# Two macaron layers on one core: softmax division moved ahead of the transposes in the second attention, and the last mixture-of-experts stage reordered

## The chip, the cores and the metric

The kernel runs on one core of a Trainium2 chip. Its engines are TensorE (PE, matrix products and transposes into PSUM), VectorE (DVE), ScalarE (ACT), GpSimd (POOL, which here also issues the indirect DMAs) and SyncE (SP, which issues plain DMAs). Each engine works through its own instruction queue in order; semaphores hold an instruction until what it reads is there. The metric is the device time of one execution in microseconds (us), lower is better.

## The reference, cut to what matters

Input x is 8 x 512 tokens of 256 float32 values. Six residual steps follow each other, each on the layer norm of x; the change lies in the last two.

```python
x = x + 0.5 * _L0_ffn_ref(_layernorm(x), ...)
x = x + _L0_attn_ref(_layernorm(x), ...)
x = x + 0.5 * _L0_ffn_ref(_layernorm(x), ...)
x = x + 0.5 * _L1_ffn_ref(_layernorm(x), ...)
x = x + _L1_attn_ref(_layernorm(x), ...)
x = x + 0.5 * _L1_ffn_ref(_layernorm(x), ...)

def _L1_attn_ref(x, w_q, w_k, w_v, w_o):        # 16 heads of 64
    q, k, v = (einsum('bsd,hdk->bhsk', x, w) for w in (w_q, w_k, w_v))
    weights = softmax(einsum('bhqk,bhmk->bhqm', q, k) / 8, axis=-1)
    z = einsum('bhqm,bhmk->bhqk', weights, v)
    return x + concat_heads(z) @ w_o

def _L1_ffn_ref(x, gate_w, w1, w2, w3, ws1, ws2, ws3):
    scores = softmax(x @ gate_w.T)              # 16 experts in 4 groups
    # the two best groups by their best score, then the four best experts in them
    y = sum over the 4 experts e of scores[e] * (silu(x @ w1[e]) * (x @ w3[e])) @ w2[e]
    return y + (silu(x @ ws1) * (x @ ws3)) @ ws2
```

## The kernel before, in words

x stays in SBUF as 32 tiles of 128 tokens (`TT` = 32); four tiles (`QT`) are one sequence of 512 tokens. `D` = 256, `CH` = 512. Both stages below are scheduled by hand: the order in which the Python emits instructions is the order in each engine's queue.

**Second attention (`_attn1`, 2174 to 3409 us).** 64 chunks `n`, each two heads of one sequence (`b, c = divmod(n, 8)`). The loop runs over half chunks `g`; each emits, in this order: the scaling of the chunk before (`scale`), the transposes of two exponential tiles of the half before (`turn`, L1130, four transposes each into a PSUM bank of tag "m", evicted to `eT` by ScalarE for the first head and VectorE for the second), some pieces of side work from the list `todo` (layer norms, gathers and additions of the FFN before, routing of the FFN after), one of the q or k projections of the next chunk (`side`, L1088), two more `turn`s, then `scores`, and then a filler (`fill`): `products` of the chunk before (L1157) in the first half, and in the second half value projections (`value`, L1077), output projections (`project`, L1172), the transposed input of the next sequence (`columns`) or gate logits of the next FFN. `scores` makes two PSUM tiles of 128 x 1024 (L1110), negates the row maximum on VectorE (L1116), and lets ScalarE write the exponentials `ex` and their row sums (L1119). The division comes last: `reciprocals` takes 1/sum, ScalarE spreads it over 64 columns for each head (`wide`, L1138), `spread` transposes that with four TensorE transposes (L1144) and copies it to `rs` (L1148), and `scale` multiplies the product `zp` by `rs` (L1164). Tag "m" has three banks, used in turn by tp, pq, pv, yp, rp and the gate's tiles.

**Last FFN (`ffn1_after`, class `Joint`, from the attention's end).** `LAST` = 20, 12: the routing of the first 20 token tiles (part 0) is done inside the attention, as pieces; their rows are sent by GpSimd (`send`, L1857, four indirect DMAs a tile) into slots ordered by expert. The other 12 tiles (part 1) are routed at the start of this stage: tiles 20 to 27 have their logits from the attention, tiles 28 to 31 (group g = 7) get norm, transposes (`columns`) and `logits` first. `routing` is a generator; `advance(steps, n)` emits up to n of its pieces, and a piece that yields "turn" ends the call. After it, 48 sends for part 1.

The expert work is a pipeline of 72 entries of two slot tiles (`tile_steps`): at step i it emits `hide(i-2)` (L2073), `back(i-3)` (L2087), `turn(i)` (L2058) and `give(i-4)` (L2095), with evictions alternating between VectorE and ScalarE, a load of `xs` from the slots (L2040) and a store of `ys` (L2103). The first 32 entries hold rows of part 0 alone, the others wait for all sends. Expert weights are picked by a register, so a `hide` waits for all of w13. From step `begin` on, `fetched` emits the combination: GpSimd gathers four rows a token (`gather`, L2010, four a tile, buffers for four tiles in all, then a memset of `pause`), and VectorE adds them to x with the coefficients (`add`, L1614), three tiles behind the gather. After the steps a `Pump` runs the shared expert in 32 units (two hidden and two output units for each group of four tiles) and spreads the remaining half tiles of `fetched` over them. A tile of x goes out once both parts are added.

`expert_weights` loads w1, w3 and w2 by groups of four experts through SP; w1 and w3 land interleaved in `w13`, in pieces of 128 values (512 bytes). `ln_root` takes the norm's square root on ScalarE, `ln_guess` by arithmetic on VectorE.

Of the kernel before, what the change touches and what calls it, by code (L numbers as in the profile page):

```python
# [19 lines left out]
P = 128  # L20
# [49 lines left out]
class Kernel:  # L70
# [124 lines left out]
    def ln_guess(self, pool, stats, t0, n):  # L195

# [11 lines left out]
        for i in range(3):  # L208
            u = small("u")
            nc.vector.tensor_tensor(u, y, y, ALU.mult)  # L210
            nc.vector.scalar_tensor_tensor(u, u, -0.5, v, ALU.mult, ALU.mult)
            new = stats[1][:, t0 : t0 + n] if i == 2 else small("y", bufs=2)
            nc.vector.scalar_tensor_tensor(new, u, 1.5, y, ALU.add, ALU.mult)
            y = new

# [820 lines left out]
    def _attn1(self, ctx, weights, one, after):  # L1036
# [61 lines left out]
        def scores(n, half):  # L1098
# [4 lines left out]
            sps = []  # L1103
# [9 lines left out]
            for i, sp in enumerate(sps):  # L1113
# [3 lines left out]
                ex = ch["ex", qt] = work.tile([P, 2, CH], F32, name="ex", bufs=4)  # L1117
                for j in range(2):
# [3 lines left out]
                    )  # L1122

# [9 lines left out]
        def reciprocals(n):  # L1133
            ch = chunk[n]
            rec = work.tile([P, QT, 2], F32, name="rec", bufs=2)
            nc.vector.reciprocal(rec, ch["sums"])
            ch["wide"] = work.tile([P, QT, 2, DK1], F32, name="wide", bufs=1)
            nc.scalar.copy(ch["wide"], bc(rec, 3, DK1))  # L1138

        def spread(n):  # L1140
            ch = chunk[n]
            rp = bank("rp")
            for qt in range(QT):
                nc.tensor.transpose(  # L1144
                    rp[:, qt * P : qt * P + P], ch["wide"][:, qt].rearrange("p h d -> p (h d)"), self.ident
                )
            ch["rs"] = work.tile([P, CH], F32, name="rs", bufs=1)
            nc.scalar.copy(ch["rs"], rp)  # L1148
# [13 lines left out]
        def scale(n):  # L1162
            zn = work.tile([P, CH], F32, name="zn", bufs=11)
            nc.vector.tensor_tensor(zn, chunk[n]["zp"], chunk[n]["rs"], ALU.mult)  # L1164
# [29 lines left out]
        def roots(ranges):  # L1194
            ys = []

            def first():
                for stats, t0, n in ranges:
                    ys.append(self.ln_root(pool, stats, t0, n))

            def second():
                for (stats, t0, n), y in zip(ranges, ys):
                    self.ln_rest(pool, stats, t0, n, y)
            return [first, second]
# [75 lines left out]
        side(0, 1)  # L1280
        for g in range(2 * N + 1):
# [3 lines left out]
            if half == 0 and n < N:  # L1285
                todo += listed(n)
            if half == 1 and n > 0:
                scale(n - 1)
            if g > 0:
                turn(m, 2 * mh, 0)  # L1290
                turn(m, 2 * mh, 1)
            if half == 0 and n > 0:
                reciprocals(n - 1)
            pieces(1)
            if n + 1 < N:
                side(n + 1, half)
# [3 lines left out]
            if half == 0 and n > 0:  # L1300
                spread(n - 1)
            if n < N:
                scores(n, half)
# [8 lines left out]
                for piece in fill(n, half):  # L1312
                    piece()
            else:
                products(n - 1)
        scale(N - 1)
# [4 lines left out]
        for i in range(QT):  # L1321
            project(B - 1, i)
            self.ln_mean(self.late, after.stats, (B - 1) * QT + i)

# [137 lines left out]
class Grouped:  # L1462
# [194 lines left out]
    def expert_weights(self, groups=range(4)):  # L1657
        nc, w = self.k.nc, self.k.w
        for g in groups:
            es = slice(g * 4, g * 4 + 4)  # L1660
            nc.sync.dma_start(
                out=self.w13[:, es, :, 0:INTER], in_=w["w1"][es].rearrange("e (c p) i -> p e c i", p=P)
            )
            nc.sync.dma_start(
                out=self.w13[:, es, :, INTER:], in_=w["w3"][es].rearrange("e (c p) i -> p e c i", p=P)
            )
            nc.sync.dma_start(out=self.w2[:, es], in_=w["w2"][es].rearrange("e p d -> p e d"))
# [160 lines left out]
class Joint(Grouped):  # L1828
# [23 lines left out]
    def send(self, h, t, row):  # L1852
# [3 lines left out]
        for r in range(TOPK):  # L1856
# [6 lines left out]
            before = self.sent[-2:-1]  # L1863
# [6 lines left out]
            self.of_part[h].append(inst)  # L1870

    def routing(self, h, lg, pool, row_psum):
# [3 lines left out]
        HT = self.parts[h]  # L1876
        GS = E1 // N_GROUPS

        score = pool.tile([P, HT, E1], F32, name="score")
# [21 lines left out]
        hots = pool.tile([P, TOPK, HT, E1], F32, name="hots")  # L1901
        yield from k.topk(pool, masked, E1, TOPK, hots)

        chosen = pool.tile([P, E1, HT], F32, name="chosen")
# [9 lines left out]
        carry = pool.tile([P, E1, HT], F32, name="masked")  # L1914
# [5 lines left out]
        inc = pool.tile([P, E1, HT], F32, name=f"left{E1}")  # L1920
# [103 lines left out]
    def tile_steps(self):  # L2024
# [25 lines left out]
        def turn(j):  # L2050
# [9 lines left out]
            k.evict(st[j]["xT"][:, :n], tp[:, :n], j)  # L2060
# [22 lines left out]
        def back(j):  # L2083
# [5 lines left out]
            k.evict(st[j]["aT"][:, :n], tp[:, :n, :P], j)  # L2089

        def give(j):
# [9 lines left out]
            k.evict(ys[:, :n], yp[:, :n], j + 1)  # L2101
# [12 lines left out]
        return load, step, len(where) + 4, known  # L2114

# [181 lines left out]
def ffn1_after(k, f, out):  # L2297
# [4 lines left out]
    with ExitStack() as ctx, k.tc.manual_schedule(engines={E.PE, E.DVE, E.Activation, E.Pool, E.SP}):  # L2302
        f.enter(ctx)
        a = f.parts[0]
        load, step, total, known = f.tile_steps()
        f.expert_weights(range(1))
        for j in range(4):
            load(j)
        f.expert_weights(range(1, 4))
        f.shared_weights()  # L2310
        g = TT // QT - 1
        for i in range(3):
            step(i)
        k.ln_guess(f.route, f.stats, g * QT, QT)
        f.normal(g)
        f.columns(g)
# [3 lines left out]
        steps = f.routing(1, f.lg1, f.route, f.row_psum)  # L2320
# [20 lines left out]
        begin, at, ends = known + 3, 0, 2 * (len(order) + 3)  # L2341
        rest = list(range(g)[::-1])
        for i in range(total):
            if i >= 3:
                step(i)
            if not sending:
                sending = not advance(steps, 4)
                if i < 2:
# [140 lines left out]
```

## Time and profile before

| what | us |
|---|---|
| runs: median of 3 (lowest, highest) | 3820.96 (3817.65, 3825.62) |
| profiled execution | 3822.71 |
| its span | 3821.0 |
| TensorE, VectorE, ScalarE, GpSimd busy | 3583.2, 1860.9, 1451.8, 1244.2 |
| second attention | 2174 to 3409 |
| last FFN, expert steps | 3409 to 3705 |
| last FFN, shared expert and rest of the gathers | 3705 to 3821 |

How to read it: the span is the profiled execution without what lies around it (1.7 us). A busy time is the union of an engine's instructions; matrix products are pipelined, so the time that one takes from the queue is read from start to start. In a windows view each line gives a stretch, its length, each engine's busy time with the number of instructions, the TensorE clock that was granted (1.00 is full), the DMA engines' share and GB/s. In a timeline a line gives start, length, engine, source line, operation, tiles, and in brackets the idle time before it with what ended it.

### The profile page before, as it was taken

What the parts mean: (1) busy time and instruction counts of PE and PEld (TensorE: products, weight loads), DVE (VectorE), ACT (ScalarE), POOL (GpSimd) and SP (SyncE); (2) the same over time, 40 slices, a digit from 0 to 9 for tenths busy, and PEclk for the clock granted to TensorE, in tenths of its full rate; (3) what the DMA queues carried; (4) which work ended last, traced back from release to release, by engine and by line L of the source; (5) the groups of instructions that cost most, each with busy time, mean ns of one, the idle gap of its engine ahead of it and who ended that gap; (6) DMA issues with size and microseconds to landing.
All of it is one profiled execution on the core that took longest, in us unless ns stands there. A gap on an engine that the chain in (4) does not pass through costs nothing.

```text
span 3821.0 us, 51805 instructions
## 1 busy us (share of the span) xinstructions
PE 3583.2 (94%) x18293; PEld 2235.2 (58%) x18293; DVE 1860.9 (49%) x4500; ACT 1451.8 (38%) x2922; POOL 1244.2 (33%) x1142
## 2 busy tenths in 40 slices
PE   4999999999996899998989999999999999988988
PEld 1566664555553566666678745555555555557865
DVE  6212205665655312116535566666556567546355
ACT  3222223444444222221123355555555555532321
POOL 2333235343331333333763312220000002714177
PEclk7999999999998899998999999999999999999989
DMA  5355442000113233324467401000000000135564
GB/s 194 97 139 146 109 103 85 23 18 23 29 34 96 49 69 78 71 41 134 135 219 236 135 18 31 28 26 1 1 1 1 1 1 23 72 113 185 163 182 130
DMA packets 258173, 309.32 MB, mean 81 GB/s; under 512 B 34048, under 2 KB 227968, under 8 KB 257664
## 3 DMA queue, kind: packets, MB, share of 16 engines
q1 hardware_dynamic: 182144, 177.78, 14.8%
q0 software_dynamic: 49152, 101.24, 10.7%
q10 hardware_dynamic: 26624, 27.00, 2.1%
q8 instruction: 151, 2.47, 0.3%
q14 instruction: 102, 0.84, 0.1%
HBM read 159.51 MB, written 138.02 MB: 78 GB/s over the span
## 4 chain that ended last, share of the span: by engine, by line
PE 37%; issue 8%; POOL 6%; DMA 2%; DVE 1%; ACT 0%; POOLq 0%; DVEq 0%; SPq 0%; ACTq 0%
PE sp L1110 6%; PE tp L1130 6%; PE pq L1088 6%; PE zp L1157 6%; PE pv L1077 3%; PE yp L1172 3%; POOL slots_d L1493 3%; PE hs L1786 2%; POOL yg L2010 2%; PE hs L2073 1%; PE yps L1808 1%; POOL slots_d L1857 1%; PE rp L1144 1%; DMA yg<-ys_d,slot 1%; PE yps L2095 1%
## 5 line engine op out<-in xcount | busy, mean ns | idle before, releaser
L521 PE MATMUL hp<-exT,w 128*128 128x512 f32 x1024 | 453.4, 597 | 0.7 <-DVE exT L509 0.7
L552 PE MATMUL op<-w,hid 128*128 128x256 f32 x2048 | 451.9, 379 | 0.0
L1119 ACT ACTIVATE ex<-sp,nmax 128x512 f32<-128x512 f32 x512 | 345.1, 686 | 238.8 <-DVE nmax L1116 238.7
L552 PEld LDWEIGHTS op<-w,hid 128*128 128x128 f32 x2048 | 386.8, 190 | 64.1 <-issue 14.4
L557 DVE TENSOR_TENSOR ob<-op,b 128x256 f32<-128x256 f32 x128 | 54.4, 425 | 642.8 <-PE op L552 555.3
L1116 DVE TENSOR_REDUCE nmax<-sp 128x2 f32<-128x1024 f32 x256 | 301.6, 1220 | 81.4 <-PE sp L1110 81.4
L531 POOL DMA_INDIRECT acc_d<-ob,idx x128 | 201.7, 1576 | 419.3 <-ACT ob L558 353.2
L812 DVE CUSTOM_DVE_ANT_0 junk<-sp,mask 128x128 bf16<-128x128 f32 (+3 forms) x512 | 251.2, 491 | 166.4 <-PE sp L803 142.3
L521 PEld LDWEIGHTS hp<-exT,w 128*128 128x128 f32 x1024 | 192.8, 191 | 221.5 <-issue 216.7
L1130 PEld LDWEIGHTS tp<-ident,ex 128*128 128x128 f32 x2048 | 233.8, 141 | 144.7 <-issue 84.7
L525 ACT ACTIVATE hid<-hp,b 128x512 f32<-128x512 f32 x256 | 175.9, 687 | 317.0 <-PE hp L521 317.0
L1130 PE MATMUL tp<-ident,ex 128*128 128x128 f32 x2048 | 272.9, 275 | 6.6 <-ACT ex L1119 4.1
L1110 PE MATMUL sp<-qk,qk 64*128 64x512 f32 x1024 | 254.4, 615 | 0.0
L1601 POOL DMA_INDIRECT yg<-ys_d,slot x128 | 129.6, 1013 | 359.2 <-DVE x L1614 267.0
L1088 PE MATMUL pq<-xnT,wide 128*128 128x512 f32 x512 | 244.1, 600 | 1.2 <-ACT xnT L250 0.8
L252 DVE COPY eT<-tp 128x512 f32<-128x512 f32 x256 | 177.1, 692 | 138.7 <-PE tp L1130 138.5
L1157 PE MATMUL zp<-eT,v 128*64 128x512 f32 x1024 | 234.0, 598 | 0.0
L250 ACT COPY eT<-tp 128x512 f32<-128x512 f32 x256 | 149.8, 585 | 220.1 <-PE tp L1130 220.1
L492 POOL DMA_INDIRECT ex<-xn_d,idx x128 | 131.5, 1027 | 297.8 <-DVE idx L483 263.6
L558 ACT ACTIVATE ob<-ob,gate 128x256 f32<-128x256 f32 x128 | 65.0, 508 | 413.9 <-DVE ob L557 413.9
L1059 POOL TENSOR_TENSOR x<-x,xn 128x1024 f32<-128x1024 f32 x8 | 18.9, 2360 | 544.1 <-DVE xn L1054 544.1
L855 ACT ACTIVATE ex<-st 128x1024 f32<-128x1024 f32 x160 | 155.1, 1022 | 95.1 <-PE st L848 95.1
(432 smaller groups left out, 6024.6 us busy)
## 6 DMA issues: line engine op xcount, KB each, us to landing
xs<-slots_d SPq DMA_DIRECT2D x149, 256.0 KB, 2.9
ys_d<-ys SPq DMA_DIRECT2D x149, 256.0 KB, 2.9
w<-in_W SPq DMA_DIRECT2D x32, 1024.0 KB, 5.2
slots_d<-zero ACTq DMA_DIRECT2D x7, 2304.0 KB, 12.8
w_sb<-in_w SPq DMA_DIRECT2D x24, 512.0 KB, 7.6
xn_d<-xn SPq DMA_DIRECT2D x16, 512.0 KB, 3.1
acc_d<-x SPq DMA_DIRECT2D x16, 512.0 KB, 4.4
x<-acc_d SPq DMA_DIRECT2D x16, 512.0 KB, 7.0
```

The costliest lines, as they stand in the source:

```text
L252: self.nc.vector.tensor_copy(out, in_)
L521: nc.tensor.matmul(hp, lhsT=w1[:, c, f * P : f * P + P], rhs=exT[e][:, c, h * CH : h * CH + CH], start=(c == 0), stop=(c == DC - 1),)
L525: nc.scalar.activation(hid[h][:, f, :], hp, AF.Gelu, bias=b1[:, e, f : f + 1])
L531: inst = nc.gpsimd.indirect_dma_start(out=acc_d[:, :], out_offset=bass.IndirectOffsetOnAxis(ap=idx[:, e, st : st + 1], axis=0), in_=ob, in ...
L552: nc.tensor.matmul(op, lhsT=hid[h][:, f, i * P : i * P + P], rhs=w2[:, f, :], start=(f == 0), stop=(f == FC - 1),)
L812: nc.vector.tensor_tensor_reduce(out=junk[:, :wd], in0=sps[h // 2][:, h % 2, at : at + wd], in1=mask[:, S - wd :], scale=1.0, scalar=NEG, ...
L1088: nc.tensor.matmul(pp, lhsT=(wq, wk)[a][:, k, c * P : c * P + P], rhs=xnT[b][:, k, :], start=(k == 0), stop=(k == DC - 1),)
L1110: nc.tensor.matmul(sp[:, j, :], lhsT=q[r, qt * P : qt * P + P], rhs=k[r, :], start=True, stop=True)
L1116: nc.vector.tensor_reduce(nmax, sp, AX.X, ALU.max, negate=True)
L1119: nc.scalar.activation(ex[:, j, :], sp[:, j, :], AF.Exp, bias=nmax[:, j : j + 1], accum_out=ch["sums"][:, qt, j : j + 1],)
L1130: nc.tensor.transpose(tp[:, k, :], ch["ex", qt][:, j, k * P : k * P + P], self.ident)
L1157: nc.tensor.matmul(zp[DK1 * j : DK1 * j + DK1, :], lhsT=v[b, h][:, k, at : at + DK1], rhs=ch["eT"][:, j, k, :], start=(k == 0), stop=(k == ...
```

## The change

**Attention.** The exponentials themselves are divided, before they are transposed: `divide(n, qt)` takes 1/sum of a row tile's two heads and multiplies the two `ex` tiles (128 x 512) in place, by the row's scalar. VectorE does both; in chunks that are `shared` (n up to 22, and from 47 until part 0 is routed) ScalarE does the first. `reciprocals` and `spread` go, and `scale` becomes a copy of `zp` on ScalarE. In `scores` the division of the first tile stands between the two tiles' exponentials; that of the second stands behind the filler. Behind a half without a filler, `side` comes ahead of `turn`. Norms inside the attention use the arithmetic root, in three pieces.

**Last FFN.** The choice of experts becomes a function `choose` of its own, and tiles 20 to 27 go through it in the attention's last batch and its closing projections (results kept in a buffer of the gathers, `kept`); the stage's own `choose` then sees four tiles, and the joint part of the routing still sees all 12. While that runs, `lean` gives all pipeline evictions to ScalarE. Weights: w1 and w3 come as one array laid out as in SBUF, w13 of three groups ahead of the first loads, then the fourth, w2 in two pieces, the shared weights. Sends of part 1 wait for the third last transfer instead of the second last, have a memset behind each tile, and begin with tiles 28 to 31. `begin` moves from `known + 3` to `known + 5`, and the pump emits three half tiles in four units, the rest behind it.

```diff
@@ ln_guess becomes a generator ln_guesses: yield after each of its three rounds
@@ _attn1
+            for qt, sp, nmax, ex in exps:
                 for j in range(2):
                     nc.scalar.activation(
                         ex[:, j, :], sp[:, j, :], AF.Exp,
                         bias=nmax[:, j : j + 1], accum_out=ch["sums"][:, qt, j : j + 1],
                     )
+                if qt == 2 * half:
+                    divide(n, qt, shared)
...
-        def reciprocals(n):
-            ch = chunk[n]
-            rec = work.tile([P, QT, 2], F32, name="rec", bufs=2)
-            nc.vector.reciprocal(rec, ch["sums"])
-            ch["wide"] = work.tile([P, QT, 2, DK1], F32, name="wide", bufs=1)
-            nc.scalar.copy(ch["wide"], bc(rec, 3, DK1))
-
-        def spread(n):
...
+        def divide(n, qt, shared):
             ch = chunk[n]
+            rec = work.tile([P, 2], F32, name="rec", bufs=4)
+            nc.vector.reciprocal(rec, ch["sums"][:, qt])
+            ex = ch["ex", qt]
+            for j in range(2):
+                if shared and j == 0:
+                    nc.scalar.mul(ex[:, j, :], ex[:, j, :], rec[:, j : j + 1])
+                else:
+                    nc.vector.tensor_scalar(ex[:, j, :], ex[:, j, :], rec[:, j : j + 1], None, ALU.mult)
...
-            nc.vector.tensor_tensor(zn, chunk[n]["zp"], chunk[n]["rs"], ALU.mult)
+            nc.scalar.copy(zn, chunk[n]["zp"])
...
+            if g == 2 * (N - NC) + 4:
+                after.kept()
+                early = [
+                    after.choose(
+                        after.lg1[:, t : t + QT], Cut(front.pool, a), after.score1[:, t : t + QT], after.hots1[:, :, t : t + QT]
+                    )
+                    for t in (0, QT)
+                ]
+                todo += [each(advance, early[0], 2)] * 13
...
+            for one_of in ("side", "turn") if not filled else ("turn", "side"):
+                if one_of == "turn" and g > 0:
+                    turn(m, 2 * mh, 0)
+                    turn(m, 2 * mh, 1)
+                    pieces(1)
+                if one_of == "side" and n + 1 < N:
+                    side(n + 1, half)
...
+                shared = n <= one.parts[1] + 2 or n >= NC * groups + 7 and not flags["routed"]
+                scores(n, half, shared)
...
+                filled = bool(filler)
+                divide(n, 2 * half + 1, shared)
...
+        advance(early[1], 11)
...
             self.ln_mean(self.late, after.stats, (B - 1) * QT + i)
+            advance(early[1], 6)
@@ expert_weights
-            nc.sync.dma_start(
-                out=self.w13[:, es, :, 0:INTER], in_=w["w1"][es].rearrange("e (c p) i -> p e c i", p=P)
-            )
-            nc.sync.dma_start(
-                out=self.w13[:, es, :, INTER:], in_=w["w3"][es].rearrange("e (c p) i -> p e c i", p=P)
-            )
-            nc.sync.dma_start(out=self.w2[:, es], in_=w["w2"][es].rearrange("e p d -> p e d"))
+            nc.sync.dma_start(out=self.w13[:, es], in_=w["w13"][:, es])
+            if back:
+                nc.sync.dma_start(out=self.w2[:, es], in_=w["w2"][:, es])
@@ Joint.send
-            before = self.sent[-2:-1]
+            before = self.sent[-2:-1] if h == 0 else self.sent[-3:-2]
...
+        if h == 1:
+            nc.gpsimd.memset(self.pause, 0.0)
@@ tile_steps, three evictions of this kind
-            k.evict(st[j]["xT"][:, :n], tp[:, :n], j)
+            k.evict(st[j]["xT"][:, :n], tp[:, :n], j | self.lean)
@@ ffn1_after
-        f.expert_weights(range(1))
+        f.expert_weights(range(3), False)
         for j in range(4):
             load(j)
-        f.expert_weights(range(1, 4))
+        f.expert_weights(range(3, 4), False)
+        f.back_weights()
         f.shared_weights()
         g = TT // QT - 1
-        for i in range(3):
+        for i in range(2):
             step(i)
         k.ln_guess(f.route, f.stats, g * QT, QT)
         f.normal(g)
+        step(2)
         f.columns(g)
...
-        steps = f.routing(1, f.lg1, f.route, f.row_psum)
+        f.lean = 1
+        steps = f.routing(1, f.lg1, f.route, f.row_psum, f.parts[1] - QT)
+        advance(steps, 1)
...
-        begin, at, ends = known + 3, 0, 2 * (len(order) + 3)
+        begin, at, ends = known + 5, 0, 2 * (len(order) + 3)
...
-                sending = not advance(steps, 4)
+                sending = not advance(steps, 6 if i < 7 else 3)
...
-                    for t in range(f.parts[1]):
+                    f.lean = 0
+                    f.pause = f.route.tile([P, CH], F32, name="pause")
+                    tokens = list(range(f.parts[1]))
+                    for t in tokens[-QT:] + tokens[:-QT]:
+                        if t % QT == 0 and t < tokens[-QT]:
+                            f.normal((a + t) // QT)
+                            rest.remove((a + t) // QT)
                         f.send(1, t, f.xn[:, a + t, :])
...
-            while at < ends and (at - from_) * units < (ends - from_) * done_units:
+            units += 1
+            if at < ends and 4 * (at - from_) < 3 * units:
                 fetched(at)
                 at += 1
```

## The prediction, made before the changed kernel had run

> **What bounds the kernel now.** I read the windows view first (busy time of each engine by stretch), because the shares over the whole span mix stages with different limits.
>
> ```profile
> core 0: us, PE busy (x) PEld busy (x) DVE busy (x) ACT busy (x) POOL busy (x), PEclk, DMA share, GB/s
> 2624.00:2774.00 150.00, 150.00 (x729) 82.14 (x727) 85.21 (x133) 77.72 (x182) 7.18 (x5) 1.00 0.00 1
> 3074.00:3224.00 150.00, 145.53 (x692) 77.79 (x688) 112.38 (x206) 77.66 (x180) 13.31 (x9) 1.00 0.01 3
> ...
> 3409.00:3432.00 23.00, 11.73 (x48) 9.53 (x47) 6.46 (x24) 3.42 (x5) 0.00 (x0) 0.68 0.62 179
> 3432.00:3470.00 38.00, 25.74 (x115) 20.61 (x115) 32.45 (x103) 9.65 (x18) 3.03 (x3) 0.84 0.26 78
> ```
>
> In the attention (2174 to 3409 us) TensorE is busy all the time at full clock; VectorE has 65 us in 150 free. TensorE time taken out there comes off the span, as long as nothing new makes it wait. The second stage, from 3409 us, is different: TensorE works 11.7 of 23 us and 25.7 of 38, at granted clocks 0.68 and 0.84. The waits behind that, from TensorE's timeline:
>
> ```profile
> 3417.48 3.49 PE L2073 MATMUL hs<-w_sb,xT 128*128 x8 [7.07 <-DMA w_sb<-in_w]
> ...
> 3425.29 2.20 PE L1679 MATMUL tp<-ident,wide 128*128 128x128 f32 x8 [3.89 <-DVE wide L1484]
> ...
> 3445.12 0.69 PE L2087 MATMUL tpa<-ident,as 128*128 128x128 f32 x2 [8.09 <-DVE aT L252]
> ...
> 3552.88 1.11 PE L2058 MATMUL tpx<-ident,xs 128*128 128x128 f32 x4 [7.16 <-DMA xs<-slots_d]
> ```
>
> Weights, layer norm, VectorE full of routing, and the sends are late in turn. The last stretch has another bound, seen in the gathers' source line:
>
> ```profile
> L2010 POOL DMA_INDIRECT yg<-ys_d,slot x128: 1006/1012/1277, 3622.2 to 3813.7; - x128
> ```
>
> 128 gathers take 191.5 us. One tile of four is 4 x (1.01 + 0.30 issue) + 0.54 memset + 0.17 = 5.95 us; 32 tiles make 190.4. So GpSimd is full from 3622.2 to the end, and the end is the first gather plus 199 us. TensorE's waits after 3622 cost nothing; those before it move the end.
>
> **The change, attention.** Removed per chunk (64 chunks): the four transposes of L1144. From the timeline:
>
> ```profile
> 2705.81 0.64 PE L1144 MATMUL rp<-ident,wide 128*128 128x128 f32 x4
> 2706.38 1.99 PE L1110 MATMUL sp<-qk,qk 64*128 64x512 f32 x8
> 2708.30 3.65 PE L1157 MATMUL zp<-eT,v 128*64 128x512 f32 x16
> 2711.88 1.09 PE L1130 MATMUL tp<-ident,ex 128*128 128x128 f32 x8
> ```
>
> Start to start, rp takes 0.57 us: 64 x 0.57 = 36.5 us gone. Also gone are ScalarE's two copies (0.62 and 0.59) and VectorE's product zn (0.69) and reciprocal (0.19). Added: four reciprocals of 128x2 (about 0.16, as the 128x4 one), a ScalarE copy zn (0.59), and eight multiplications of 128x512 in place. No row is that form. Nearest: L387, tensor_scalar 128x256 with one pointer scalar, 354 ns. The int32 tensor_scalars of 128x4 (170) and 128x256 (287) give 0.464 ns an element, so 354 + 256 x 0.464 = 473: I take 0.48 us. Bounds: 0.35, and 0.69 (copy 128x512 from PSUM). The instruction order of the changed kernel has 126 of the 512 on ScalarE, 0.62 as L1138.
>
> VectorE per 18.8 us chunk: 85.21/150 x 18.78 = 10.7 now; 10.7 - 0.88 + 0.64 + 8 x 0.48 = 14.3 of 18.2 after. It fits, but latency decides. From scores (time 0): first maximum 1.17, both maxima to 3.53, first exponentials 2.43 to 3.88 with the accumulator read, reciprocal to 4.1, two multiplications to 5.2. TensorE comes for these tiles at 1.92 (scores) + 3.58 (products, values or projection, all near 3.55) = 5.50. Cover is 0.3 us; formerly the tiles were ready at 3.9. Where it tears, by scheduling the queues of a chunk by hand:
> - Unshared chunks with value projections (12): evictions of pv now stand behind the first division, and the second division behind them; bank "m" (three buffers) comes free at 6.67, wanted at 6.4: 0.3 each, 4 us.
> - Shared chunks (31): ScalarE's multiplication waits for the reciprocal with the next exponentials queued behind it, and zn and the first eviction behind those: 8.43 against 8.15, 0.28 each, 9 us.
> - Chunks where norm or routing pieces (1 to 5 us of VectorE) lie between the two divisions, about 14 by the order: 0.7 each, 9 us.
> Sum 22 (between 0 and 45, twice as much if a multiplication is 0.69): net -14.5 us. Layer-norm roots by arithmetic instead of Sqrt take table loads (1.28 each) from ScalarE: 0, TensorE covers them at 150.00 of 150 today; early routing of eight tiles (two times some 40 operations near 0.2, 8 us) lies in the last batch, where VectorE has 67 of 150 us free, and behind the 14 us of closing projections: 0, at worst 2.
>
> **The change, last FFN.** TensorE work from the projections' end (3409.2) to the first gather: turn 52 x 0.43, hide 50 x 1.73, back 49 x 0.22, give 48 x 0.87 = 161.5 us, gate 4: 165. The first gather stands at +213, so 48 us are lost: 31 in waits, the rest half clock and landing. After:
> - Weights. Before the first hide lay 4.19 MB of w13, 1.57 of w2, 1.05 of xs, issued from 3390.9, landed 3417.4: 257 GB/s. Now 4.19 + 1.05 = 5.24 MB, 20.4 us, landed 3411.3 against 3410.4 wanted. 7.1 becomes 1 to 2. (The old order back: 7.1.) SP now issues w2 and the shared weights behind all w13: w2 lands 8 us later, near 3420, first used by give(0) in step 4, near 3426: 0. In the first FFN the same DMAs are early: 0.
> - Norm ahead of step 2: VectorE is through at +6, hide covers it: 3.9 becomes 1.
> - Routing of 4 tiles, not 12, up to the choice: operations of 0.2 instead of 0.36, six yields a step = 2.6 us, inside a step of 3.25, and with `lean` the evictions are ScalarE's (1.94 a step). 8.1 becomes 0; the joint part (scan, slots, coefficients on 12 tiles, normals) overfills three steps: 5 remain.
> - Slots are ready near +31 (formerly +56.6). 48 sends, three flying, at 1.27 plus 12 memsets of 0.71 = 70 us (82 before): done at +104, with landing and load +107. TensorE comes to step 32 near +113: 7.2 becomes 0 to 3.
> - Landing of ys 5, clock after the remaining waits 5.
> Together 20 to 22: first gather at +187, gain 26 (12 to 34).
> - Pace. First adds two steps later, then three half tiles in four units. Adds of tile t free the buffer of gather t+4; in the loop they come one per 4.9 us, in the pump one per 2.67 units x 2.9 = 7.8 us, against 5.95 for GpSimd, but start 15 us ahead of need and fall behind only past tile 26: 0 (at worst 4). The scores kept in a `yg` buffer are read for the last time before the first send, long before gather 2 wants it: 0.
>
> Sum against the profiled execution (3822.7 us, span 3821.0): 3822.7 - 14.5 - 26 = 3782; the median of the runs is 1.75 lower: **3781**.
>
> **Rivals.**
> - No new stalls in the attention, all FFN waits gone: 3822.7 - 36.5 - 34 = 3752. For it: VectorE has 4 us a chunk free. Against: the evictions above are in queue order.
> - Multiplications at 0.69, or double stalls: 45 us against 36.5 saved, +8; 3822.7 + 8 - 26 = 3805. Against: the slope 0.464.
> - The FFN keeps its lost time (sends or weights are late by another wait): 3822.7 - 14.5 - 5 = 3803. For: first gather waits on DMA 73.6 us.
> - GpSimd and VectorE hinder each other. The same tensor_scalar form took 401 to 1399 ns (L694) beside GpSimd work. In chunks 54 to 62 sends keep GpSimd busy 105 of 150 us; 8 multiplications x half a send (0.49) x 0.7 = 2.7 us a chunk, nine chunks, half of it hidden: +12, 3793. The Trainium skill (SBUF - State Buffer, "shared port pair") states that such an operation in its two-port mode and a GpSimd operation exclude each other for a whole instruction; by that rule this holds, only where GpSimd works. The range 401 to 1399 agrees.
> - **Slower**: the chain scores, maximum, exponentials, reciprocal, multiplication misses its cover in all 128 half chunks. Place: the transposes of `turn`. Cover ends at 5.50. A chain of 6.2 us stalls 0.7 x 128 = 90: 3822.7 + 90 - 36.5 - 26 = 3850. It decides from 5.50 + (36.5 + 26)/128 = 6.0 on. Against: my 5.2 is added from rows; five hand-overs would each have to cost 0.15 more.
>
> **How the numbers follow.** Forecast 0.48, no stalls 0.2, double stalls 0.11, FFN keeps its time 0.08, GpSimd 0.07, slower 0.06. 0.2% (7.6 us) is about what a measurement can tell from no change. Faster takes all but the slower case and some of the two near 3804: 0.9; same 0.04; slower 0.06. The likeliest case alone spans 3767 to 3795 (its stalls 10 to 30, its FFN gain 18 to 32). The range takes in most of the first rival and those near 3805: 3756 to 3808.
>
> **What would show it.** rp gone and TensorE above 99% busy in the attention, chunks of 18.2 to 18.6 us; multiplications near 0.48; waits of `turn` on VectorE or ScalarE under 0.5 us. First gather near +187 after the last projection, and 199 us from it to the end. Wrong would be: chunks of 18.8 or more; gathers with idle GpSimd between them, the pace being the new bound; a first gather still near +210.

## The result, and the profile after

The changed kernel takes 3790.06 us (median of 4 runs, 3786.41 to 3791.66) beside 3821.99 for the kernel before on the same chip: ratio 0.9912, 95% interval 0.9900 to 0.9924, so 32 us or 0.9% faster. 3781 was forecast. The profiled execution took 3789.19 us, its span is 3787.5. On another chip the sign turned round (runs 9 and 10), and runs 5 to 8, on a third, point the same way.

The windows view of the changed kernel, the two attention stretches first, then the start of the last FFN in steps of 20 us from the last projection on:

```profile
core 0: us, PE busy (x) PEld busy (x) DVE busy (x) ACT busy (x) POOL busy (x), PEclk, DMA share, GB/s
2624.00:2774.00 150.00, 149.21 (x699) 79.40 (x696) 114.30 (x226) 71.78 (x177) 7.59 (x5) 1.00 0.00 1
3074.00:3224.00 150.00, 146.35 (x679) 77.52 (x680) 125.17 (x257) 88.06 (x199) 18.81 (x15) 1.00 0.02 6
3398.00:3418.00 20.00, 16.31 (x97) 13.70 (x96) 12.46 (x54) 10.18 (x18) 0.00 (x0) 1.00 0.48 161
3418.00:3438.00 20.00, 17.99 (x98) 15.22 (x97) 17.79 (x64) 8.71 (x20) 3.37 (x3) 1.00 0.46 145
3438.00:3458.00 20.00, 18.18 (x99) 15.70 (x98) 13.93 (x33) 5.96 (x13) 15.52 (x19) 1.00 0.72 224
```

TensorE is still nearly full in the attention (149.21 of 150), and VectorE went from 85 to 114 us in that stretch. In the last FFN TensorE now works 52.5 of the first 60 us at full clock; before, it was 11.7 of 23 and 25.7 of 38 at 0.68 and 0.84.

A plain chunk of the attention, from the timeline of TensorE:

```profile
2792.69 1.04 PE L1139 MATMUL tp<-ident,ex 128*128 128x128 f32 x8
2793.66 1.99 PE L1115 MATMUL sp<-qk,qk 64*128 64x512 f32 x8
2795.58 3.65 PE L1160 MATMUL zp<-eT,v 128*64 128x512 f32 x16
2799.16 1.09 PE L1139 MATMUL tp<-ident,ex 128*128 128x128 f32 x8
```

and VectorE's at the same place:

```profile
2797.58 0.17 DVE L1145 RECIPROCAL rec<-sums 128x2 f32<-128x2 f32 x1 [0.38 <-ACT ex L1126]
2797.78 0.89 DVE L1151 TENSOR_SCALAR ex<-ex,rec 128x512 f32<-128x512 f32 x2
```

rp is gone; scores follow the transposes directly. Two multiplications take 0.89 us, and the second tile is through at 2798.67, 5.0 us after the scores started; TensorE comes back at 5.5.

The waits of TensorE in the last FFN, as before from its timeline:

```profile
3402.45 1.97 PE L2102 MATMUL hs<-w_sb,xT 128*128 x8 [1.07 <-DVE u L215]
...
3405.96 0.66 PE L1689 MATMUL tp<-ident,wide 128*128 128x128 f32 x4 [0.68 <-ACT xnT L1692]
...
3426.45 0.59 PE L1955 MATMUL pp<-chosen,tri 128*128 128x192 f32 x2 [1.24 <-DVE left L1953]
...
3512.93 0.89 PE L2087 MATMUL tpx<-ident,xs 128*128 128x128 f32 x4 [2.26 <-DMA xs<-slots_d]
```

No wait for weights is left (7.07 before): all of w13 has landed at 3396.8, and the 1.07 us ahead of the first hide are put down to VectorE's arithmetic for the norm (L215). The norm's wait is 0.68 (3.89), the routing's longest 1.24 (8.09), the sends' 2.26 (7.16).

Where the 33.5 us of span went. The starts are read from the timelines: first and last scores, last projection `yp`, first and last send of part 1, first gather, last instruction.

| | before | after | difference |
|---|---|---|---|
| first to last scores of the attention | 1210.7 | 1197.7 | -13.0 |
| end of the projections, from the span's start | 3408.9 | 3398.4 | -10.5 |
| from there to the first send | 56.6 | 35.6 | |
| first to last send of part 1 | 82.1 | 69.9 | |
| end of projections to first gather | 213.3 | 185.4 | -27.9 |
| first gather to the end | 198.7 | 203.6 | +4.9 |

-10.5 - 27.9 + 4.9 = -33.5, the difference of the spans. Of the 13.0 us that the attention gains up to its last scores, 2.5 are lost again outside: 0.7 before the first scores, and 1.9 between the last scores and the end of the projections (26.7 us instead of 24.7). There the division of the last chunk has too little TensorE work beside it to be covered:

```profile
3376.90 3.48 PE L1139 MATMUL tp<-ident,ex 128*128 128x128 f32 x16 [0.87 <-DVE ex L1151]
```

In the kernel before, these 16 transposes take 2.6 us, with no wait ahead of them. With the old division (run 1) the stretch has 25.0 us.

### The profile page after: what moved, and what is told of

Read it like the earlier page. It is cut to its first block, busy times and chain, and to the rows that moved or that the text cites. A ratio compares the mean times of both kernels' runs of the same rounds, so it can differ in the third digit from the quotient of the medians.

```text
span 3787.5 us, 51747 instructions
## 1 busy us (share of the span) xinstructions
PE 3546.3 (94%) x18037; PEld 2197.5 (58%) x18037; DVE 2042.3 (54%) x5170; ACT 1474.6 (39%) x2966; POOL 1257.2 (33%) x1154
## 4 chain that ended last, share of the span: by engine, by line
PE 36%; issue 6%; POOL 5%; DVE 5%; DMA 2%; ACT 2%; POOLq 0%; DVEq 0%; SPq 0%; ACTq 0%
PE sp L1115 6%; PE tp L1139 5%; PE pq L1093 5%; PE zp L1160 5%; PE hs L2102 3%; POOL slots_d L1501 3%; PE pv L1082 2%; PE yp L1175 2%; PE hs L1796 2%; POOL yg L2039 2%; ACT ex L1126 1%; PE yps L2124 1%; PE yps L1818 1%; DVE ex L1151 1%; DVE nmax L1121 1%
## 5 line engine op out<-in xcount | busy, mean ns | idle before, releaser
L1151 DVE TENSOR_SCALAR ex<-ex,rec 128x512 f32<-128x512 f32 x386 | 190.0, 521 | 9.0
L1064 POOL TENSOR_TENSOR x<-x,xn 128x1024 f32<-128x1024 f32 x8 | 18.9, 2364 | 529.6 <-DVE rec L1145 380.4
```

Of the source, the lines that this page charges most:

```text
L1151: nc.vector.tensor_scalar(ex[:, j, :], ex[:, j, :], rec[:, j : j + 1], None, ALU.mult)
```

## The experiments

The runs came to lie on three chips: runs 1 to 4 on one where the kernel before takes 3820.41 us, as fast as the one of the result (both are called the first chip below); runs 5 to 8 on one where it takes 3929.07, and runs 9 to 12 on one where it takes 3931.25. On the last two (the second and the third chip) the FFN ahead of this attention (called the first FFN), which the change does not touch, is already 70 to 100 us longer (first scores of the second attention at 2247 to 2271 us instead of 2174). Each ratio is to the kernel before on the same chip; across chips only stages are compared.

### Run 1: the old division, all else changed

```diff
-                    divide(n, qt, shared)
...
+            reciprocals(n - 1)
...
+            spread(n - 1)
...
-            nc.scalar.copy(zn, chunk[n]["zp"])
+            nc.vector.tensor_tensor(zn, chunk[n]["zp"], chunk[n]["rs"], ALU.mult)
```

> The changed kernel with the division of the kernel before (reciprocals, spread, scale, the old order of the half chunk); the last FFN, the early choice and the arithmetic roots stay. Theory A (the attention gained what the chunk pitches show, 13 us from first to last scores, 10 to 12 with the projections): 3800 to 3803 us, chunk pitches 18.6 to 18.8, rp back at 0.48 a chunk. Rival B (the gain in the attention is that of the Sqrt table loads, not of rp): within 3 us of the changed kernel.

Measured: 3799.3 us, ratio 0.9939 (0.9927 to 0.9951), 9 us over the changed kernel: close to theory A, and outside rival B. First to last scores 1206.2 us; a plain half chunk pair, start of scores to start of scores, is back from 9.12 + 9.19 to 9.12 + 9.66. So the division gives some 9 of the 32 us. But rival B has a part too: with the old division this attention is still 4.5 us shorter than that of the kernel before (1210.7). 4.3 of them lie in chunks 48 to 54, and the half chunks of 10.54 and 10.69 us in chunks 48 and 52 are 9.51 and 9.66 here. In the kernel before, ScalarE loads the table of the square root there, its copy of a projection stands behind that,

```profile
3185.94 1.28 ACT L192 ACT_TABLE_LOAD   x1
3187.35 0.58 ACT L1094 ACTIVATE qk<-pq 128x512 f32<-128x512 f32 x1
```

and TensorE waits:

```profile
3188.08 0.63 PE L1144 MATMUL rp<-ident,wide 128*128 128x128 f32 x4 [0.88 <-DVE eT L252]
```

The arithmetic root, which run 1 keeps, has no table load. The other 2.2 us, in chunks 53 and 54, were not traced to a cause.

### Run 2: the pieces of side work behind the second division

```diff
-                pieces(2 - half)
...
                 divide(n, 2 * half + 1, shared)
+                pieces(2 - half)
```

> The changed kernel with the pieces of side work that lay between the two divisions of a half chunk moved behind the second. Theory A (the stalls of 17 us that are left are VectorE work standing ahead of the second division): the slow chunks of norms (c = 0 and 2 of sequences 3 to 5, 0.7 to 0.9 too long each) and of routing come down to 18.3, 6 to 10 us less, 3780 to 3784. Rival B (they come from banks that an eviction frees late, whatever the order): within 2 us of 3790, or the stalls move to the half chunk behind.

Measured: 3796.84, ratio 0.9944 (0.9929 to 0.9959), no gain, rather a loss: rival B's second case. The half chunk of 10.03 us in the third chunk of sequences 3 to 5 became 9.12, but the stalls came back elsewhere: the first chunk of these sequences takes 19.1 instead of 18.9, and half chunks with routing pieces in sequence 6 take 10.86 instead of 9.12, 12.98 instead of 12.04 and 14.59 instead of 13.33. The pieces cost wherever they stand between what TensorE waits for; moving these moves the stall.

### Run 3: one half tile of the combination in each unit of the pump

```diff
-            if at < ends and 4 * (at - from_) < 3 * units:
+            if at < ends and 1 * (at - from_) < 1 * units:
```

> The changed kernel with one half tile in every unit of the pump instead of three in four. Theory A (GpSimd starves 8.5 us for additions emitted too late): waits of the gathers on L1622 gone, first gather to end 198 to 199 instead of 203.7, 4 to 6 us less, 3784 to 3786. Rival B (earlier additions block VectorE on gathers, TensorE is late and the end with it): 3790 or more, TensorE ending after the last gather.

Measured: 3785.05, ratio 0.9904 (0.9889 to 0.9918); first gather to end 195.7 instead of 203.6 us. The view of the gathers' source line, first the changed kernel:

```profile
L2039 POOL DMA_INDIRECT yg<-ys_d,slot x128: 1007/1012/1274, 3583.8 to 3781.3; - x128
...
  DVE x L1622: 7.6, 4
```

then this run:

```profile
L2039 POOL DMA_INDIRECT yg<-ys_d,slot x128: 1011/1015/1272, 3587.4 to 3777.0; - x128
...
  DVE x L1622: 1.0, 6
```

The line below gives for how long GpSimd stood idle until an addition of VectorE freed a gather's buffer: 7.6 us in four places became 1.0. The change's pace emits the additions late near the end, as theory A has it. The time itself is 5 us lower, within the scatter of both kernels; the idle time is what shows it.

### Run 4: no memset between the gathers

```diff
-        nc.gpsimd.memset(self.pause, 0.0)
```

> The changed kernel without the memset behind each tile of gathers in the last FFN. Theory A (GpSimd's instruction time is the bound from the first gather to the end: 0.71 us a tile): 32 x 0.71 = 22.7 us less on GpSimd; the additions and the DMA wait of the third last gather then bind, so 8 to 18 us less, 3772 to 3782. Rival B (three transfers in flight are the bound, the memset lies in their shade): within 3 us of 3790, waits of the gathers on their own DMA grow by what the memset took.

Measured: 3789.46, ratio 0.9913 (0.9900 to 0.9926), no gain in the time: a miss for theory A. The stage itself, first gather to end, is 198.3 us instead of 203.6 (203.0 and 206.2 in runs 2 and 1, which do not touch it); the attention and what lies ahead of it, which this run does not touch either, were longer by about as much. The gathers' line of this run:

```profile
  DVE x L1622: 18.7, 13
  DMA yg<-ys_d,slot: 9.9, 17
```

By the expectation's price the memsets took 22.7 us; some 5 of them are gained, and 11 go into waiting for additions (18.7 us instead of 7.6). So "GpSimd is full" was not the bound by itself: the memset lies mostly in the shade of the additions' pace.

### Run 5: the choice of experts for eight tiles back in the last FFN

```diff
-                todo += [each(advance, early[0], 2)] * 13
...
-        advance(early[1], 11)
...
-        steps = f.routing(1, f.lg1, f.route, f.row_psum, f.parts[1] - QT)
+        steps = f.routing(1, f.lg1, f.route, f.row_psum, 0)
```

> The changed kernel with the early choice undone: no routing of tiles 20 to 27 in the attention, all 12 chosen in the last FFN, the rest as changed. Theory A (the early choice takes VectorE work off the critical start of the stage): some 20 operations at 0.36 come back, 7 us of VectorE in five steps, part hidden: first gather 3 to 8 us later after the projections' end, attention up to 2 us shorter: 3791 to 3797. Rival B (lean evictions and the sends hide the routing anyway): within 2 us of 3790.

Measured on the second chip: 3947.11, ratio 1.0047 (1.0022 to 1.0073). The first send comes 40.9 us after the projections, against 37.9 in run 8 on the same chip and 37.3 for the changed kernel (run 9, third chip). First to last scores 1199.7 against 1199.8 and 1199.2. So the early choice is worth 3 to 3.6 us in the FFN, and is free in the attention; with `lean` and six pieces a step most of the old 8.1 us wait is gone even without it (the longest left ahead of the sends is 1.24).

### Run 6: the old order and layout of the expert weights

```diff
-            nc.sync.dma_start(out=self.w13[:, es], in_=w["w13"][:, es])
+            nc.sync.dma_start(out=self.w13[:, es, :, 0:INTER], in_=w["w1"][es].rearrange(...))
+            nc.sync.dma_start(out=self.w13[:, es, :, INTER:], in_=w["w3"][es].rearrange(...))
...
-        f.back_weights()
```

> The changed kernel with the weights of the kernel before: w1, w3, w2 by groups in 512-byte rows, first group ahead of the first loads. Theory A (the first hide waited 7.1 us for weights): a wait of 5 to 8 us on w_sb before the first hide is back, clock halved behind it; part of it is taken up by the wait for the sends: 3793 to 3799. Rival B (the norm and the seam set the start): within 2 us of 3790.

Measured on the second chip: 3952.84, ratio 1.0062 (1.0038 to 1.0087). TensorE's timeline has the wait for weights back:

```profile
3503.30 3.75 PE L2100 MATMUL hs<-w_sb,xT 128*128 x8 [5.85 <-DMA w_sb<-in_w]
```

Counted from the end of the projections, the first send comes at +45.2 us instead of +37.9 (run 8, same chip) or +37.3 (run 9), the first gather at +237.0 instead of +233.2 or +231.6: 4 to 8 us for the weights.

### Run 7: sends in twos

```diff
-            before = self.sent[-2:-1] if h == 0 else self.sent[-3:-2]
+            before = self.sent[-2:-1]
```

> The changed kernel with the sends of part 1 waiting for the second last transfer again (the memsets stay). Theory A (TensorE stands 2.3 us at the first tile of part 1 for the sends): 48 sends take 82 to 90 us instead of 70, the wait at the first load of part 1 grows to 12 to 22 us and the first gather moves by as much: 3800 to 3810. Rival B (transfers, not their order, are the limit): within 3 us of 3790.

Measured on the second chip: 3897.23, ratio 0.9931 (0.9910 to 0.9953), some 40 to 55 us below runs 5, 6 and 8 on that chip. The sends take 80.8 us instead of 65 to 66, the wait at the first entry that needs them is 9.63 us instead of 2.2 to 2.4; and yet the first gather comes at +193.8 us, not at +233 to +237. That had to be set against the changed kernel itself: runs 9 and 10.

### Run 8: every multiplication on VectorE

```diff
-                shared = n <= one.parts[1] + 2 or n >= NC * groups + 7 and not flags["routed"]
+                shared = False
```

> The changed kernel with all 512 multiplications on VectorE, none on ScalarE. Theory A (VectorE has room: 14 of 18.3 us a chunk; half chunks shared with ScalarE cost 9.16 against 9.12): same or 1 to 2 us less in plain chunks, 2 to 6 us more where additions or routing crowd VectorE: 3788 to 3795. Rival B (VectorE is full in the shared chunks): 0.5 us a chunk in 31 chunks, 3800 to 3810.

Measured on the second chip: 3938.55, ratio 1.0024 (1.0004 to 1.0043); first to last scores 1199.8 us, beside 1199.2 with the sharing (run 9). First half chunks that were shared go from 9.16 to 9.12 us, and as much is lost where routing and norm pieces lie. Which engine multiplies does not matter here.

### Runs 9 and 10: the changed kernel and the same with sends in twos, on one chip

Run 9 has no edit; run 10 has that of run 7.

> The changed kernel without any edit, as the measure for the three runs beside it. Theory A (the 32 us gained are a property of the kernel): ratio to the kernel before 0.991 +- 0.002 on any chip; from the end of the last projection to the first gather +185, 48 sends in 66 to 70 us, no wait over 3 us of TensorE while they run. Theory B (the sends in threes leave the loads and stores of the tiles too little on a chip whose transfers are slow, as the kernels in which threes were kept showed in the second group): on such a chip first gather at +230 or more, waits of 4 to 13 us in tpa, ratio 1.00 or above; on a chip like the first both theories give the same numbers.

> Two sends in flight instead of three, against the changed kernel run beside it. Theory A (threes are worth the 10 to 12 us by which the 48 sends get shorter, less what TensorE's tiles hide): 80 to 82 us of sends instead of 66 to 70, the wait at the seam 8 to 10 us instead of 2.3, first gather +7 later, time 5 to 9 us longer than the changed kernel's. Theory B (threes starve the loads and stores where transfers are slow): on such a chip the first gather comes 35 to 45 us earlier than in the changed kernel and the time is 30 to 45 us shorter; on a chip like the first, as theory A.

Measured on the third chip: the changed kernel 3939.72, ratio 1.0026 (1.0006 to 1.0045); with twos 3902.09, ratio 0.9938 (0.9914 to 0.9961). The first gather stands at +231.6 with threes and +193.7 with twos. Theory B holds: on this chip the third transfer in flight costs 38 us, more than all that the change gains. The windows view while the sends run, with threes:

```profile
3537.00:3557.00 20.00, 14.24 (x76) 12.00 (x75) 10.41 (x27) 3.79 (x9) 15.84 (x18) 0.95 0.53 175
3557.00:3577.00 20.00, 12.64 (x33) 8.30 (x31) 3.10 (x7) 1.23 (x3) 16.15 (x18) 0.59 0.41 135
3577.00:3597.00 20.00, 5.32 (x15) 3.53 (x15) 0.85 (x2) 1.55 (x3) 15.92 (x19) 0.50 0.33 109
```

and with twos:

```profile
3529.00:3549.00 20.00, 18.29 (x99) 15.82 (x98) 15.18 (x35) 5.97 (x13) 13.40 (x16) 1.00 0.66 213
3549.00:3569.00 20.00, 20.00 (x112) 17.79 (x111) 11.18 (x23) 6.73 (x15) 12.10 (x15) 1.00 0.73 238
3569.00:3589.00 20.00, 20.00 (x113) 17.76 (x112) 7.41 (x15) 6.71 (x16) 12.36 (x14) 1.00 0.73 240
```

With threes TensorE, VectorE and ScalarE all but stop (15, 2 and 3 instructions in 20 us) while GpSimd sends on at its pace, and the granted clock falls to 0.50. What they wait for is seen by laying TensorE's timeline of run 9

```profile
3568.84 2.07 PE L2124 MATMUL yps<-w_sb,aT 128*128 x4
3573.45 3.78 PE L2102 MATMUL hs<-w_sb,xT 128*128 x8 [2.54 <-DVE xT L257]
3590.31 0.69 PE L2116 MATMUL tpa<-ident,as 128*128 128x128 f32 x2 [13.07 <-issue]
```

beside ScalarE's:

```profile
3579.09 0.58 ACT L255 COPY ys<-yps 128x512 f32<-128x512 f32 x1 [12.18 <-remote]
3586.96 0.38 ACT L2108 ACTIVATE sgs<-hs 128x256 f32<-128x256 f32 x1 [7.28 <-remote]
```

The products `yps` end at 3570.9 by the trace, and their copy starts at 3579.1; `hs` ends at 3577.2, and its activation starts at 3587.0: 8.2 and 9.7 us later, while `as` on VectorE follows `sgs` within 0.41 us as always. Of the 15 waits of VectorE and ScalarE that TensorE ended between 3534 and 3600, the median is 2.1 us from the product's end to the reader's start. In run 10 none of 40 has more than 0.4 us while the sends run, and on the first chip, with the same three in flight, none of 52 more than 0.1 (`yps` ends at 3473.00, its copy starts at 3473.04). The profile models the ends of products, so the rows do not tell whether the product or its signal is late. What holds TensorE's results back on these chips is not shown by any row, and was not tried further. Nor were twos tried on the first chip: what threes are worth there is not known.

### Run 11: pace of run 3, no memset, and side pieces ahead of the turn once

```diff
-                filled = bool(filler)
+                filled = bool(filler) and (n, half) != (3, 1)
```

and the edits of runs 3 and 4.

> Three edits read in two stages. Pace of one half tile a unit and no memset between the gathers: theory A (once the additions come early, GpSimd's own instructions bind: 1.31 us a gather, 5.25 a tile instead of 5.95): first gather to end 176 to 183 us, time 12 to 20 us below the pace alone (3785 there), near 3768. Theory B (transfers or the additions bind and the memset lies in their shade, as when it alone was taken out): 193 to 200 us, time within 4 us of the pace alone. Side pieces ahead of the turn in chunk 4 after the filler that has only columns: theory A (the turn came 1.9 us too early there): that half chunk 9.2 instead of 11.19 us, 2 us off; theory B (the projection of q and k is what is late): 11.0 or more.

Measured on the third chip: 3933.2, ratio 1.0011 (0.9991 to 1.0030), 6.5 us below run 9 with overlapping intervals. First gather to end 218.7 us against 221.4: theory A falls here too, but on this chip the gathers wait 33.8 us for additions (31.3 in run 9), so that it says nothing of the first chip, where the two edits were not tried together. The side piece is plain: the half chunk goes from 11.03 us (run 9) to 8.83. The changed kernel's TensorE there:

```profile
2241.88 1.09 PE L1074 MATMUL tpn<-ident,xn 128*128 128x128 f32 x8
2244.86 1.09 PE L1139 MATMUL tp<-ident,ex 128*128 128x128 f32 x8 [1.88 <-ACT ex L1149]
```

The filler has only 0.9 us of transposes, so the turn comes 1.88 us too early; with the projection put between, it is covered.

### Run 12: two more multiplications ahead of the first division

```diff
             nc.vector.reciprocal(rec, ch["sums"][:, qt])
             ex = ch["ex", qt]
+            if qt % 2 == 0:
+                for _ in range(2):
+                    nc.vector.tensor_scalar(ex[:, int(shared), :], ex[:, int(shared), :], self.ones[:, 0:1], None, ALU.mult)
```

> Two more VectorE multiplications (by one) of 128x512 ahead of the division of the first query tile of each half chunk, 0.44 us each: the chain to the transposes is 0.88 us longer. Theory A (the trace after: the first multiplied tile is ready 0.9 us before its transposes can start, the second 0.9 before its own): plain half chunks stay at 9.12 to 9.25, attention 0 to 15 us longer, most of it where pieces lie between the divisions. Theory B (the cover in the prediction, 0.3 to 0.5 us): 0.4 to 0.6 a half chunk more, some 114 of them filled: 45 to 70 us longer, plain half chunks 9.5 to 9.7. Theory C (the copies behind the division are late as well, so it counts whole): 0.88 a half chunk, 100 us or more.

Measured on the third chip: 3995.75, ratio 1.0170 (1.0145 to 1.0194); first to last scores 1254.0 against 1199.2, +54.8 us. The size is theory B's, the place is not: a plain half chunk whose filler is the products goes only from 9.12 to 9.20 us, as theory A has it, and one whose filler is value projections from 9.19 to 9.95. TensorE's timeline there,

```profile
2820.51 0.63 PE L1139 MATMUL tp<-ident,ex 128*128 128x128 f32 x4
2821.42 0.66 PE L1139 MATMUL tp<-ident,ex 128*128 128x128 f32 x4 [0.28 <-DVE v L1086]
```

and VectorE's:

```profile
2819.88 0.89 DVE L1156 TENSOR_SCALAR ex<-ex,rec 128x512 f32<-128x512 f32 x2
2820.68 1.28 DVE L1086 COPY v<-pv 128x512 f32<-128x512 f32 x2
```

The transposes wait for the copies of `v` that stand behind the divisions on VectorE and hold the PSUM bank. So there are two covers in these chunks: 0.8 us for the chain to the transposes after products (0.88 less the 0.08 that showed), and 0.12 us (0.88 less 0.76) for the copies of `v`. The second is nearly used up. In the shared chunks, where ScalarE does the first multiplication, the half chunk with value projections goes to 9.55, and 0.52 us are covered.

The plain half chunks with value projections make 14 of the 54.8 us, and plain ones with products or output projections 10. The other 31 lie in the half chunks at the attention's two ends and in those that side work had already made longer. The first two half chunks of sequences 3 to 5, for example, grow by 0.91 each: nothing was covered there any more, as theory C has it.

## Why the prediction was right

**The time.** 3790 lies in the range, 9 us above the point; the likeliest case held, faster, with each of its two parts near its sum: attention -13.0 (forecast -14.5), first gather 28 us earlier from the projections on (forecast 26). In the profiled execution 7.0 us are lacking (3789.2 against 3782): 4.9 in the last stretch, 2.5 outside the scores, 1.5 in the attention, less 1.9 that the first gather is ahead of the forecast. That the number held has luck in it: on the third chip the same kernel is 0.3% slower than the kernel before, by a mechanism that the forecast does not have (below).

**rp, 36.5 forecast, 30.7 measured.** A term mis-sized. A chunk lost 0.48 us, not 0.57. Before, the last transposes took 0.88 us from start to start ahead of rp, and the same group ahead of the scores takes 0.97 (2792.69 to 2793.66). The forecast took rp's own stretch; it should have taken 0.88 + 0.57 - 0.97 = 0.48, which the other half chunk of the trace before shows.

**Norm roots, 0 forecast, 4.5 measured.** "TensorE covers them at 150.00 of 150" was read from plain chunks. In chunks 48 and 52 the table loads were not covered, and run 1 has the 4.5 us without the new division.

**New stalls, 22 forecast, 22 measured, but in other places.** 64 x 0.48 + 4.5 - 13.0 = 22.2. That the sum agrees is luck, for its parts do not. Shared chunks cost 0.04 each, not 0.28, though ScalarE's multiplication took 0.72 and not 0.62; chunks with value projections cost nothing, not 0.3, with the mechanism real but 0.12 us short of showing (run 12). Pieces between the divisions, forecast at 9 us for 14 chunks, cost some 12: 0.8 in the first chunk of sequences 3 to 5, and some 9 us in all from the fifth chunk of sequence 5 on, where the routing lies. (Counting from 0, sequence 5 begins with chunk 40.) Six more stalls, 0.75 in each of chunks 8, 18 and 49 and 0.9 in each of chunks 26, 34 and 42, come from a GpSimd operation (below). Two stalls were not seen at all: 2.7 us in chunk 3, where the turn follows a short filler (run 11), and 1.1 in chunk 0.

**The multiplication, 0.48.** Right: median 486 ns. A few are longer. GpSimd's timeline of the changed kernel,

```profile
2666.23 2.36 POOL L1064 TENSOR_TENSOR x<-x,xn 128x1024 f32<-128x1024 f32 x1 [92.91 <-DVE rec L1145]
```

and VectorE's:

```profile
2666.25 3.03 DVE L1151 TENSOR_SCALAR ex<-ex,rec 128x512 f32<-128x512 f32 x2
```

The pair that takes 0.89 elsewhere takes 3.03 when it starts 0.02 us behind a GpSimd operation of 2.36. One of the two multiplications takes 2.62 us here and in two other chunks; in three more chunks, where one starts 1.1 us into the same operation, it takes 1.58. Each of the six ends some 0.3 us behind the GpSimd operation, and these are the six chunks named above; with the pieces moved (run 2), no multiplication takes more than 751 ns, and all six stalls are gone. The Trainium skill (SBUF — State Buffer, Terms, "shared port pair") states that VectorE and GpSimd share a pair of ports, which one instruction holds to its end while the other is blocked. The six agree with it; GpSimd's `tensor_scalar`s of 128x256 (L1492) do not show it: of 19 multiplications of VectorE that start inside one, 12 take 480 to 489 ns and the longest 711. And the rival that put 12 us on the sends fell: in 3224 to 3374 us, with GpSimd busy 103.76 of 150, the 66 multiplications have a median of 486 and a longest of 740 ns. It is one form of GpSimd operation (the addition in L1064) that holds VectorE up for long here, not the sends.

**Weights, norm, routing, seam.** All four waits went as forecast: 7.1 to nothing (1 to 2 forecast), 3.9 to 0.7 (1), the routing's 8.1 to 3.8 in four pieces (5), 7.2 to 2.3 (0 to 3). Run 6 gives 4 to 8 us for the weights (7.1 forecast). The early choice, counted among the causes of the routing's gain, is worth only 3 to 3.6 of it (run 5).

**Sends in threes, 70 us forecast.** Right in length: 69.9, and 65 to 66 on the other chips. That three in flight could slow the other engines was no step of the forecast. On the chip of the trace TensorE works 59.35 of 60 us from 3442 on, while they run; on the third chip threes decide the sign (runs 9 and 10), and on the second, where the changed kernel was not run without an edit, runs 7 and 8 point the same way. That the result comes from a chip where they do no such harm is luck.

**Pace, 0 forecast, "at worst 4".** Wrong by +4.9: additions come late near 3729 to 3753 us, where the forecast had them 15 us ahead (run 3). And "GpSimd is full from the first gather to the end" was true only as a sum: taking out 22.7 us of memsets shortened the stage by 5.3 us and the time by nothing (run 4).

**The slower rival.** It was to decide from a chain of 6.0 us. The chain is 5.0; run 12 made it 5.9, and the attention lost 54.8 us, and 54.8 - 10.5 - 27.9 + 4.9 = 21 us would be left over the kernel before on the first chip. So it decides earlier than forecast, for two reasons: a second reader, the copies of `v`, has only 0.12 us of cover in unshared chunks (14 us of the 54.8 come from half chunks with value projections), and half chunks with side work had none left (most of the other 31).

## What to carry to other kernels

Price a removed group by what its neighbours take start to start with and without it; the trace before often has both. When work moves into an engine's queue, ask for every later reader of that queue how much cover it has left: the chain to the obvious reader had 0.8 us, the copy behind it 0.12, and half chunks with side work none. Put the main part of a change back alone: run 1 showed that 4.5 us of the attention's gain came from a part that had been priced at nothing. A deeper queue of indirect transfers is to be timed on more than one chip: here three in flight instead of two were part of a gain of 0.9% on one and turned -0.6% into +0.3% on another.

## What the runs showed of the hardware that was not expected

- The same kernel, and the one before, differ by 3% between chips (3820 and 3931 us for the kernel before). Where three indirect sends are in flight on the third, TensorE's results reach other engines late, by 2.1 us in the median and up to 9.7 (run 9), GpSimd's pace unchanged (1.28 us a send). The first FFN keeps three in flight before and after the change, and in run 10 TensorE works 12.62 of the 40 us from 1960 to 2000 there at clock 0.62, beside 28.84 at 0.84 on the first chip: the same sign, but twos were not tried in it.
- GpSimd's sends left VectorE's multiplications at 486 ns in the median; one form of GpSimd operation (an addition of two 128x1024 tensors, 2.36 us) held up each of the six that met it, by 1.1 or 2.1 us.
- Four transposes of 0.57 us by their own stretch were worth 0.48 us when they were taken out.
